# Inverse transforms along x of three images: one product of folded columns in place of two

## The chip, the cores and the metric

The kernel runs on one core of a Trainium2 chip. Its time is the device time of one execution in microseconds (us). The median of three runs of the kernel before is 10099.33 us (10097.6 to 10100.59). All arrays are 32-bit floats.

A core has five engines with instruction queues of their own: TensorE (PE) multiplies matrices, with its weight loads shown apart (PEld); VectorE (DVE), ScalarE (ACT) and GpSimd (POOL) work element by element; SyncE (SP) issues nearly all transfers between the chip's main memory and the core's on-chip memory. Products land in a separate accumulator memory of eight banks, called PSUM.

## The reference

Four images x of 128 channels and 128 x 128 pixels go through two layers. The first is a selective state-space layer over windows of 8 x 8 pixels. The second is a Fourier layer; only that one is touched:

```python
z = layer norm of x over the channels
Xf = jnp.fft.rfft2(z, axes=(-2, -1))                      # 128 x 65 frequencies
Uf = Xf[:, :, None, :, :] * jnp.conj(Phi)[None, None]     # 16 complex masks Phi_l
U = jnp.fft.irfft2(Uf, s=(gx, gy), axes=(-2, -1))
S = jnp.einsum('bdlxy,lhd->bhxy', U, Theta)
H = gelu(W1 S + b1)
out = W2 H + b2
return x + out
```

The kernel mixes channels before it transforms back: for each frequency it forms the sum over l of conj(Phi_l) times Theta_l Xf, and applies the inverse transform to that sum, one image of 128 channels at a time.

## The kernel before, in words

**Stages.** One core does everything in sequence: the state-space layer (0 to 7120 us, `mamba_layer`), the forward transforms (`spectra`, to 7420), the mixing with Theta and Phi (`mix`, to 9294), and then, image by image, the inverse transforms and the MLP (`images_and_mlp`, to the end). The order of instructions on each engine is that in which the program writes them; inside these stages there is no planner. SP too works strictly in order: a transfer whose source isn't ready, or whose buffer isn't free, holds up every transfer written after it.

**Mixing.** A row is one y frequency y of the 65 (KY). For each of 16 masks k, `products` multiplies the row's spectrum `xk` (columns of x frequencies as weights) by Theta_k (line 621), so that the results have the x frequency on the 128 partitions and image by channel along the free axis. Real and imaginary parts are then scaled by Phi, one number per partition, and added to `acc` (line 649 on DVE, lines 636 and 638 on ACT and POOL for the masks of `APART`). `COLS` says which x frequency each partition holds: frequencies 0 to 31, then the mirror images of 0 to 31 (128 minus the frequency, and 64 in place of the mirror image of 0), then 32 to 63, then their mirror images. So partition 32 + i holds the mirror image of partition i, and 96 + i that of 64 + i. `finish` stores each row to main memory in `sf` (line 659), 8 transfers a row: four images by two halves of the channels.

**Images and MLP.** For one image, `load_spectrum` brings the mixed spectrum back (x frequency on partitions; y frequency, real or imaginary part, channel along the free axis). `reorder` copies 16 channels at a time into `so`, laid out as minus imaginary, real, imaginary (lines 710 to 712). `along_x` transforms along x: for each channel two products are added in PSUM, one with the cosines `ix[:, :W]` (line 721) and one with the sines `ix[:, W:]` (line 722). The weights are the channel's spectrum (128 x 128) and the results have 128 y numbers (65 real and 63 imaginary parts) on partitions and the pixel x along the free axis. Four channels share a PSUM bank; ACT and DVE take turns copying banks into `px` (line 724). When all 128 channels are through, the image goes on in 32 steps of four pixels x. Each step k has `along_y` (line 735, product with `idft_y`, copied by DVE, line 736), `hidden` (line 743, W1, and line 744, gelu on ACT) and `project` (line 752, W2, and line 753, where DVE adds the bias and the layer's input). The steps are staggered: step k writes `along_y` of k + 1, `hidden` of k and `project` of k - 1. Every second step loads eight rows of the layer's input `mx` (line 730), and every second `project` stores eight rows of the result (line 755). The spectrum of the next image is loaded in two halves, one in the middle of `along_x`, one in step 0 of the MLP.

Of the kernel before, what the change touches and what calls it, by code (L numbers as in the profile page):

```python
# [13 lines left out]
F32 = mybir.dt.float32  # L14
# [20 lines left out]

COLS = np.arange(W // 2).reshape(2, 1, W // 4)
COLS = np.concatenate((COLS, np.where(COLS > 0, W - COLS, W // 2)), 1).reshape(W)


def mamba_layer(tc, d, x, x1, zb, deltas, dus, results):  # L40
# [549 lines left out]
        tc.nc.sync.dma_start(t[:, :, :, q], xf[y // YG][y % YG, :, :, q])  # L590


def mix(tc, theta, phi, xf, firsts, sf, first):

# [8 lines left out]
    with ExitStack() as ctx:  # L603
        ctx.enter_context(tc.manual_schedule())
        sb = ctx.enter_context(tc.tile_pool(name="m_sb", bufs=3, reuse_waits="tile"))
        ps = ctx.enter_context(tc.tile_pool(name="m_ps", bufs=4, space=PSUM, reuse_waits="tile"))
        nc.vector.tensor_scalar(phi[2], phi[1], -1.0, None, ALU.mult)
        rows = {y: SimpleNamespace(xk=t) for y, t in enumerate(firsts)}

# [53 lines left out]
        load(2)  # L663
        for y in range(KY):
# [8 lines left out]
        finish(KY - 1)  # L673


def load_spectrum(tc, sf, b, q, groups, t):
    for g in groups:
        tc.nc.sync.dma_start(t[:, SG[g] : SG[g + 1]], sf[b][g][:, q])


def images_and_mlp(tc, c, sp, spec, sf, x1, out):

    nc = tc.nc
    B = len(sf)
    CG, CB = HB // W, 16
    HP = P // 2
    n = WS * W  # L690
    with ExitStack() as ctx:
        ctx.enter_context(tc.manual_schedule())
        sb = ctx.enter_context(tc.tile_pool(name="i_sb", bufs=2, reuse_waits="tile"))
        ps = ctx.enter_context(tc.tile_pool(name="i_ps", bufs=2, space=PSUM, reuse_waits="tile"))
        ix, iy = c["idft_x"], c["idft_y"]
        ordered, px, rows = {}, {}, {}

        def load(b, q):
            if b < B:
                spec[b, q] = sp.tile([P, KY, 2, HP], F32, tag="s", name="s", bufs=2)  # L700
                load_spectrum(tc, sf, b, q, range(len(SG) - 1), spec[b, q])

        def reorder(b, i):

            if i == P:
                b, i = b + 1, 0
            if b < B:
                s = spec[b, i // HP][:, :, :, i % HP : i % HP + CB]
                t = ordered[b, i] = sb.tile([P, CB, 3 * KY - 2], F32, tag="so", name="so")
                nc.scalar.activation(t[:, :, :KY].rearrange("p c y -> p y c"), s[:, :, 1], AF.Copy, scale=-1.0)  # L710
                nc.vector.tensor_copy(t[:, :, KY : 2 * KY].rearrange("p c y -> p y c"), s[:, :, 0])
                nc.vector.tensor_copy(t[:, :, 2 * KY :].rearrange("p c y -> p y c"), s[:, : KY - 2, 1])

        def along_x(b, i):
            if i % CB == 0:
                reorder(b, i + CB)
                along_x.s = ordered.pop((b, i))
            p1 = ps.tile([P, CG, W], F32, tag="p1", name="p_ix")
            for k in range(CG):
                s = along_x.s[:, i % CB + k]  # L720
                nc.tensor.matmul(p1[:, k], s[:, KY:], ix[:, :W], start=True, stop=False)
                nc.tensor.matmul(p1[:, k], s[:, :P], ix[:, W:], start=False, stop=True)
            to = px[b][:, :, i : i + CG].rearrange("p x c -> p c x")
            (nc.scalar.copy if i % (2 * CG) else nc.vector.tensor_copy)(to, p1)

        def along_y(b, k):
            if k % 2 == 0:
                o = rows[b, k // 2] = SimpleNamespace(at=slice(k * CG, (k + 2) * CG))
                o.x = sb.tile([P, n], F32, tag="mx", name="mx")
                nc.sync.dma_start(o.x, x1[b][:, o.at].rearrange("c x y -> c (x y)"))  # L730
                o.u = sb.tile([P, 2, HB], F32, tag="mu", name="mu")
                o.o = sb.tile([P, n], F32, tag="mo", name="mo")
            p2 = ps.tile([P, CG, W], F32, tag="p2", name="p_iy")
            for q in range(CG):
                nc.tensor.matmul(p2[:, q], px[b][:, k * CG + q], iy, start=True, stop=True)
            nc.vector.tensor_copy(rows[b, k // 2].u[:, k % 2], p2.rearrange("p x y -> p (x y)"))

        def hidden(b, k):
            o = rows[b, k // 2]
            o.g = sb.tile([P, 2, HB], F32, tag="g", name="g")  # L740
            for m in range(2):
                ph = ps.tile([P, HB], F32, tag="ph", name="p_h")
                nc.tensor.matmul(ph, c["W1"][:, m * P : (m + 1) * P], o.u[:, k % 2], start=True, stop=True)  # L743
                nc.scalar.activation(o.g[:, m], ph, AF.Gelu, bias=c["b1"][:, m : m + 1])
            return o.g

        def project(b, k, g):
            o = rows[b, k // 2]
            hs = slice(k % 2 * HB, (k % 2 + 1) * HB)
            po = ps.tile([P, HB], F32, tag="po", name="p_o")  # L750
            for m in range(2):
                nc.tensor.matmul(po, c["W2"][:, m], g[:, m], start=(m == 0), stop=(m == 1))
            nc.vector.scalar_tensor_tensor(o.o[:, hs], po, c["b2"], o.x[:, hs], ALU.add, ALU.add)
            if k % 2:
                nc.sync.dma_start(out[b][:, o.at].rearrange("c x y -> c (x y)"), o.o)

        reorder(0, 0)
        for b in range(B):
            px[b] = sb.tile([P, W, P], F32, tag="px", name="px", bufs=1)
            for i in range(0, P, CG):  # L760
                along_x(b, i)

                if i == HP + CB:
                    load(b + 1, 0)
            along_y(b, 0)
            before = None
            for k in range(W // CG):
                if k + 1 < W // CG:
                    along_y(b, k + 1)
                g = hidden(b, k)  # L770
                if before:
                    project(b, *before)
                before = k, g
                if k == 0:
                    load(b + 1, 1)
            project(b, *before)


# [1 line left out]
def conv_kernel(ctx: ExitStack, tc: tile.TileContext, d, out):  # L780
# [3 lines left out]
    def images(name):  # L784
# [4 lines left out]
    sf = [  # L789
        [tc.dram_tile([W, 2, j - i, 2, P // 2], F32, name=f"sf_{b}_{i}") for i, j in zip(SG[:-1], SG[1:])]  # L790
        for b in range(B)
    ]
# [5 lines left out]
    with ExitStack() as stages:  # L798
        with tc.tile_pool(name="results", bufs=1, side="right") as results:
# [10 lines left out]
            def constants():  # L810
# [5 lines left out]
                m.firsts = [  # L816
                    small([B, 4 * (W // 2)], f"xk{y}").rearrange("p b (r q x) -> p b r q x", r=2, q=2) for y in range(2)
                ]

            def first_rows():  # L820
                for y, t in enumerate(m.firsts):
# [1 line left out]

            spectra(tc, d, zb, xf, zp, stores, constants, first_rows)

        sp = ctx.enter_context(tc.tile_pool(name="sp", bufs=1, side="right", reuse_waits="tile"))
        c = {}
        for k in "idft_x idft_y W1 b1 W2 b2".split():
            c[k] = sp.tile(list(d[k].shape), F32, tag=k, name=f"c_{k}")
            nc.sync.dma_start(c[k], d[k])  # L830
        spec = {(0, q): sp.tile([P, KY, 2, P // 2], F32, tag="s", name="s", bufs=2) for q in range(2)}

        def first_image(g):
            for q in range(2):
                load_spectrum(tc, sf, 0, q, [g], spec[0, q])

        mix(tc, m.theta, m.phi, xf, m.firsts, sf, first_image)
    images_and_mlp(tc, c, sp, spec, sf, x1, out)


def dft():
# [2 lines left out]
    h = w[:, :KY]  # L844

    s = w[:KY] * np.where(np.arange(KY) % (W // 2) == 0, 1, 2)[:, None] / W**2
    parts = {
        "dft_x": (h.real, -h.imag[:, 1:-1]),
        "dft_y": (h.imag, h.real, -h.imag),
        "idft_x": (w.real[COLS], w.imag[COLS]),  # L850
    }
    d = {k: np.concatenate(v, 1).astype(np.float32) for k, v in parts.items()}
    rows = np.r_[1 : KY - 1, 0, KY - 1]
# [15 lines left out]
def layout(i):  # L869
# [17 lines left out]
    d["Phi_r"], d["Phi_i"] = (i[f"L1_conv_Phi_f_{k}"].transpose(1, 0, 2)[COLS] for k in ("real", "imag"))  # L887
# [21 lines left out]
```

## Time and profile before

| | |
|---|---|
| median of three runs | 10099.33 us |
| the profiled execution | 10102.73 us |
| its span, first to last instruction | 10100.2 us |
| state-space layer | 0 to 7120 us |
| forward transforms | 7120 to 7420 us |
| mixing | 7420 to 9294 us |
| images and MLP | 9304 to 10100 us |
| PE busy in the whole span | 9084.8 us (90%) |
| DVE, ACT, POOL | 88%, 64%, 82% |

The profile is of one execution. A group row gives the line, the engine and the operation; what it writes and reads; shapes; how often; then busy time, the mean duration of one, and the engine's idle time just before them with what ended that. Matrix products follow each other so closely that their durations overlap; what one costs is the step from one to the next. A product of 32-bit numbers shows as two records. A stretch row gives busy time and number of instructions of PE, PEld, DVE, ACT and POOL in a window, the clock that PE was granted (1.00 is full), the mean busy share of the 16 DMA engines, and the rate of transfer in GB/s. DMA rows give the size of one transfer and the median time from its issue to its landing.

### The profile page before, as it was taken

Reading aid. Unit: us, or ns where it says so; the run is one execution under the profiler, and the core shown is the slowest. Engines: PE = TensorE matmul, PEld = TensorE weight load, DVE = VectorE, ACT = ScalarE, POOL = GpSimd, SP = SyncE. Lnnn points to the kernel's source line nnn. Section 1 sums busy time; section 2 is a strip of 40 time slices with the busy share of each in tenths; the row PEclk is TensorE's granted clock in tenths of the full one; section 3 lists DMA queues with packets and bytes.
Section 4 is the critical chain, followed back from the end, with each engine's and each line's share of the span. In section 5 each row is a group of like instructions: output and inputs, shape, how many; then the busy total and the mean of one; then the engine's idle time right before and its main releaser. Section 6 shows DMA issues by size and latency. Waiting matters only on the chain.

```text
span 10100.2 us, 142674 instructions
## 1 busy us (share of the span) xinstructions
PE 9084.8 (90%) x47892; PEld 4884.4 (48%) x47892; DVE 8843.0 (88%) x7100; ACT 6493.7 (64%) x12443; POOL 8238.1 (82%) x4259
## 2 busy tenths in 40 slices
PE   7888888888888888888888888888899999999999
PEld 3333333333333333333332333332799999999666
DVE  6999999999999999999999999999579999998333
ACT  5776777777777777777767777776545555554433
POOL 6898899999999989988998999999369999996000
PEclk8899999999999999999999999998899999999999
DMA  5777677777767777777776777777741111111332
GB/s 176 215 227 219 211 229 217 219 219 223 223 214 227 218 215 223 220 220 215 227 221 212 229 219 218 218 221 223 212 116 39 47 37 45 39 47 54 131 128 92
DMA packets 1173229, 1793.97 MB, mean 178 GB/s; under 512 B 369664, under 2 KB 437520, under 8 KB 1169296
## 3 DMA queue, kind: packets, MB, share of 16 engines
q1 hardware_dynamic: 1171920, 1784.71, 58.5%
q8 instruction: 380, 6.23, 0.3%
q14 instruction: 353, 2.89, 0.1%
q10 hardware_dynamic: 576, 0.14, 0.0%
HBM read 1481.41 MB, written 303.04 MB: 177 GB/s over the span
## 4 chain that ended last, share of the span: by engine, by line
PE 65%; ACT 15%; DVE 9%; DMA 6%; issue 3%; SPq 1%; POOL 1%; DVEq 0%; ACTq 0%; POOLq 0%
PE p_v L621 18%; PE p_conv L220 6%; PE p_du L400 6%; DVE hs L434 6%; DMA dr<-delta 5%; PE p_dt L245 5%; PE p_bc L235 5%; PE p_y L452 5%; DVE p_du L432 3%; ACT dA L415 3%; PE p_out L292 2%; PE ln_cen L169 2%; ACT cs L176 2%; ACT p_du L415 2%; PE p_h L743 2%
## 5 line engine op out<-in xcount | busy, mean ns | idle before, releaser
L442 POOL TENSOR_TENSOR hs<-hs,bc 128x1024 f32<-128x1024 f32 x2048 | 4811.0, 2377 | 398.0 <-DVE hs L434 347.3
L434 DVE TENSOR_TENSOR_SCAN hs<-dA,p_du 128x1024 f32<-128x1024 f32 x1600 | 3659.2, 2287 | 211.5 <-ACT dA L415 8.9
L432 DVE TENSOR_TENSOR p_du<-p_du,bc 128x1024 f32<-128x1024 f32 x1600 | 1936.3, 1210 | 194.2 <-PE p_du L400 189.5
L415 ACT ACTIVATE dA<-dr,A 128x504 f32<-128x504 f32 x3200 | 2071.7, 704 | 35.2 <-DVE hs L434 24.1
L621 PE MATMUL p_v<-theta,xk 128*128 128x128 f32 x16640 | 1864.0, 275 | 16.3 <-DMA xk<-xf 11.8
L621 PEld LDWEIGHTS p_v<-theta,xk 128*128 128x128 f32 x16640 | 1861.1, 192 | 19.2 <-issue 11.9
L649 DVE SCALAR_TENSOR_TENSOR acc<-p_v,phi,acc 128x512 f32<-128x512 f32 x2622 | 1768.0, 744 | 104.4 <-PE p_v L621 80.0
L638 POOL TENSOR_TENSOR acc<-acc,part 128x512 f32<-128x512 f32 x1408 | 1741.4, 1282 | 117.2 <-ACT part L636 110.5
L400 PE MATMUL p_du<-du,c_rsel 32*128 32x512 f32 x6400 | 1362.0, 677 | 372.1 <-DVE hs L434 371.9
L452 PE MATMUL p_y<-hs,c_ssel 128*32 128x512 f32 x8192 | 1224.6, 633 | 137.8 <-DVE yz L281 83.4
L636 ACT ACTIVATE part<-p_v,phi 128x512 f32<-128x512 f32 x1408 | 891.3, 686 | 578.7 <-PE p_v L621 572.5
L434 DVE TENSOR_TENSOR_SCAN hs<-p_du,ur 128x1024 f32<-128x1024 f32 x448 | 1019.0, 2275 | 79.1 <-ACT p_du L415 58.3
L380 POOL TENSOR_TENSOR ur<-ur,bc 128x1024 f32<-128x1024 f32 x448 | 1064.7, 2377 | 10.5 <-DMA ur<-du 10.5
L220 PE MATMUL p_conv<-tn,W_conv 128*128 128x512 f32 x2016 | 991.9, 616 | 0.0
L400 PEld LDWEIGHTS p_du<-du,c_rsel 32*128 32x128 f32 x6400 | 370.3, 192 | 1083.3 <-issue 782.6
L245 PE MATMUL p_dt<-xc,W_dt 128*128 128x512 f32 x1008 | 609.7, 735 | 40.6 <-ACT dl L256 39.2
L415 ACT ACTIVATE p_du<-dr,A 128x504 f32<-128x504 f32 x896 | 613.9, 685 | 29.1
L452 PEld LDWEIGHTS p_y<-hs,c_ssel 128*32 128x32 f32 x8192 | 184.1, 111 | 890.6 <-issue 565.9
L225 ACT ACTIVATE xc<-p_conv,b_conv 128x512 f32<-128x512 f32 x252 | 173.5, 688 | 625.8 <-PE p_conv L220 625.8
L220 PEld LDWEIGHTS p_conv<-tn,W_conv 128*128 128x128 f32 x2016 | 341.6, 189 | 446.3 <-issue 244.3
L263 POOL TENSOR_TENSOR dl<-dl,ab 128x1024 f32<-128x1024 f32 x128 | 302.8, 2365 | 299.1 <-ACT ab L260 299.1
L235 PE MATMUL p_bc<-xc,c_W_bc 128*128 128x512 f32 x1008 | 493.3, 612 | 36.0 <-ACT dl L256 36.0
(133 smaller groups left out, 9683.8 us busy)
## 6 DMA issues: line engine op xcount, KB each, us to landing
dr<-delta SPq DMA_DIRECT2D x4096, 256.0 KB, 5.2
ur<-du SPq DMA_DIRECT2D x896, 256.0 KB, 6.4
delta<-dl SPq DMA_DIRECT2D x128, 512.0 KB, 2.9
du<-du SPq DMA_DIRECT2D x128, 512.0 KB, 5.4
xf<-x SPq DMA_DIRECT2D x40, 832.0 KB, 8.8
xk<-xf SPq DMA_DIRECT2D x130, 256.0 KB, 3.7
sf<-acc SPq DMA_DIRECT2D x520, 64.0 KB, 1.7
xt<-in_x_dram SPq DMA_DIRECT2D x64, 512.0 KB, 7.4
```

What stands on the lines that cost most here:

```text
L220: nc.tensor.matmul(windows(o.pc), W_conv[:, ch, k], moved, start=(k == 0), stop=(k == K - 1))
L245: nc.tensor.matmul(o.pd, W_dt[:, k, ch * P : (ch + 1) * P], half(o.xc[:, k], h), start=(k == 0), stop=(k == 1))
L380: nc.gpsimd.tensor_tensor(fetched[s], fetched[s], both(o.bc[0], h), ALU.mult)
L400: nc.tensor.matmul(u.bank[:, j % 2], c["rsel"][p, u.i], half(u.o.du[p, u.ch], u.h), start=True, stop=True)
L415: nc.scalar.activation(u.dA[:, q, :, 1:], u.delta[:, q].rearrange("p (w t) -> p w t", t=L)[:, :, 1:], AF.Exp, scale=A[:, g : g + 1],)
L432: nc.vector.tensor_tensor(u.bu, u.bu, both(u.o.bc[0], u.h), ALU.mult)
L434: nc.vector.tensor_tensor_scan(u.hs.rearrange("p q t -> p (q t)"), u.dA.rearrange("p q w t -> p (q w t)"), u.bu.rearrange("p q t -> p (q t)"),
L442: nc.gpsimd.tensor_tensor(u.hs, u.hs, both(u.o.bc[1], u.h), ALU.mult)
L452: nc.tensor.matmul(o.py[h, ch][32 * j : 32 * j + 32], c["ssel"][:, u.i], units[s + j // 2].hs[:, j % 2], start=(u.i == 0), stop=False, ski ...
L621: nc.tensor.matmul(t[:, b], o.xk[:, b, r], theta[:, k], start=True, stop=True)
L638: nc.gpsimd.tensor_tensor(into, into, part, ALU.add)
L649: nc.vector.scalar_tensor_tensor(into, v, factor, into, ALU.mult, ALU.add)
```

## The change

A real image has a spectrum whose parts at a frequency and at its mirror image enter the same cosine and sine. For the images after the first, the two products along x are replaced by one. Its weights, `folded`, are sums of two terms: the real part of a column and the imaginary part of its mirror image, and so on, with signs. The matrix `ix[:, :W]` then holds cosines on the partitions of frequencies up to 64 and sines on those of the mirror images.

- *Phi.* On the mirrored partitions Phi_r and Phi_i change places, and a new input `sign` (+1 or -1 per partition) multiplies `phi[0]` at the start of `mix`, so that those partitions hold the spectrum times i, up to sign.
- *Stores.* The first image's two stores a row are unchanged. Those of images 1 to 3 go to new tensors `sf_b`, each [128, 4, 2, 65, 32]: quarter of the channels, real or imaginary, y frequency, 32 channels. There are still 8 transfers a row.
- *Loads.* In steps 0, 3, ..., 21 of an image's MLP, `load` brings one piece (a quarter q of the next image's channels, part r) as one transfer of 128 partitions into `s`, and part 1 - r of the same quarter, with mirrored partitions exchanged, into `mirrors[r]` as four transfers of 31, 31, 32 and 32 partitions. Partitions 0 and 32 have no partner and stay zero. Each partition's row is 65 x 32 numbers, 8,320 bytes, in one piece.
- *Folds.* Three steps later `fold` adds or subtracts the two on GpSimd and writes the result, with y frequency along the innermost axis, into `folded`, 128 channels by 128. The two parts of a quarter make 65 and 63 columns.
- *Images 1 to 3* have no `reorder`. The first image still has its two products and its reorders.
- *Memory.* `along_x` uses all eight PSUM banks in turn, the MLP writes its result into the tile that holds its input (three buffers, `mo` is gone), and pools are closed and opened after the first image's transforms. The constants of the last stage get a pool of their own; their six loads then stand on SP ahead of the stores of the first image's forward spectrum instead of behind those of the last.

```diff
+MIRROR = COLS > W // 2
+HQ = 32
...
+        nc.vector.tensor_scalar(phi[0], phi[0], sign, None, ALU.mult)
         nc.vector.tensor_scalar(phi[2], phi[1], -1.0, None, ALU.mult)
...
-                for b in range(B):
-                    for q in range(2):
-                        hs = slice(q * (P // 2), (q + 1) * (P // 2))
-                        nc.sync.dma_start(sf[b][g][:, q, at - SG[g]], o.acc[:, b, :, hs])
-                    if b == 0 and y in [k if k < KY else KY - 1 for k in SG[1:]]:
-                        first(g)
+                for q in range(2):
+                    hs = slice(q * (P // 2), (q + 1) * (P // 2))
+                    nc.sync.dma_start(sf[0][g][:, q, at - SG[g]], o.acc[:, 0, :, hs])
+                if y in [k if k < KY else KY - 1 for k in SG[1:]]:
+                    first(g)
+                for b in range(1, B):
+                    for r in range(2):
+                        nc.sync.dma_start(sf[b][:, :, r, at], o.acc[:, b, r].rearrange("p (q h) -> p q h", h=HQ))
...
+        def load(b, i):
+            if b < B and i < 2 * (P // HQ):
+                q, r = divmod(i, 2)
+                s[i] = late.tile([P, KY, HQ], F32, tag="s", name="s")
+                nc.sync.dma_start(s[i], sf[b][:, q, r])
+
+                for to, of in ((0, 32), (32, 0), (64, 96), (96, 64)):
+                    at = int(to < 64)
+                    nc.sync.dma_start(mirrors[r][to + at : to + 32], sf[b][of + at : of + 32, q, 1 - r])
+
+        def fold(b, i):
+            if b < B and 0 <= i < 2 * (P // HQ):
+                q, r = divmod(i, 2)
+                k = KY - 2 * r
+                to = folded[:, q * HQ : (q + 1) * HQ, r * KY : r * KY + k].rearrange("p c y -> p y c")
+                nc.gpsimd.tensor_tensor(to, s.pop(i)[:, :k], mirrors[r][:, :k], ALU.add if r else ALU.subtract)
+
         def along_x(b, i):
-            if i % CB == 0:
-                reorder(b, i + CB)
-                along_x.s = ordered.pop((b, i))
-            p1 = ps.tile([P, CG, W], F32, tag="p1", name="p_ix")
+            if b == 0 and i % CB == 0:
+                reorder(i + CB)
+                along_x.s = ordered.pop(i)
+
+            bank = ("p1", "p2", "ph", "po")[i // CG % 4]
+            p1 = ps.tile([P, HB], F32, tag=bank, name="p_ix").rearrange("p (c x) -> p c x", x=W)
             for k in range(CG):
-                s = along_x.s[:, i % CB + k]
-                nc.tensor.matmul(p1[:, k], s[:, KY:], ix[:, :W], start=True, stop=False)
-                nc.tensor.matmul(p1[:, k], s[:, :P], ix[:, W:], start=False, stop=True)
+                if b:
+                    nc.tensor.matmul(p1[:, k], folded[:, i + k], ix[:, :W], start=True, stop=True)
+                else:
+                    t = along_x.s[:, i % CB + k]
+                    nc.tensor.matmul(p1[:, k], t[:, KY:], ix[:, :W], start=True, stop=False)
+                    nc.tensor.matmul(p1[:, k], t[:, :P], ix[:, W:], start=False, stop=True)
...
-                o.x = sb.tile([P, n], F32, tag="mx", name="mx")
+                o.x = sb.tile([P, n], F32, tag="mx", name="mx", bufs=3)
...
-            nc.vector.scalar_tensor_tensor(o.o[:, hs], po, c["b2"], o.x[:, hs], ALU.add, ALU.add)
+            nc.vector.scalar_tensor_tensor(o.x[:, hs], po, c["b2"], o.x[:, hs], ALU.add, ALU.add)
...
+            if b == 0:
+                early.close()
+                done()
+                late = ctx.enter_context(tc.tile_pool(name="i_late", bufs=2, reuse_waits="tile"))
+                folded = late.tile([P, P, P], F32, tag="folded", name="folded", bufs=1)
+                for r in range(2):
+                    mirrors.append(late.tile([P, KY, HQ], F32, tag=f"sm{r}", name="sm", bufs=1))
+                    nc.gpsimd.memset(mirrors[r], 0.0)
             along_y(b, 0)
             before = None
             for k in range(W // CG):
+                if k % 3 == 0:
+                    fold(b + 1, k // 3 - 1)
+                    load(b + 1, k // 3)
...
-        "idft_x": (w.real[COLS], w.imag[COLS]),
+        "idft_x": (np.where(m, -w.imag[COLS], w.real[COLS]), np.where(m, w.real[COLS], w.imag[COLS])),
...
+    m = MIRROR[:, None, None]
+    d["Phi_r"], d["Phi_i"] = np.where(m, j, r), np.where(m, r, j)
+    d["sign"] = np.where(MIRROR, -1, 1).astype(np.float32)[:, None]
```

More of the change, by code (lines that the diff above doesn't have):

```diff
@@ L590, in load_row, with mix @@
         tc.nc.sync.dma_start(t[:, :, :, q], xf[y // YG][y % YG, :, :, q])
-def mix(tc, theta, phi, xf, firsts, sf, first):
+def mix(tc, theta, phi, sign, xf, firsts, sf, first):
     nc = tc.nc
@@ L673, in mix, with images_and_mlp @@
         finish(KY - 1)
[L676 to L681, printed above, removed]
+def images_and_mlp(tc, c, spec, done, sf, x1, out):
     nc = tc.nc
@@ L694, in images_and_mlp, with reorder @@
         ps = ctx.enter_context(tc.tile_pool(name="i_ps", bufs=2, space=PSUM, reuse_waits="tile"))
+        early = ExitStack()
+        so = early.enter_context(tc.tile_pool(name="i_so", bufs=2, reuse_waits="tile"))
         ix, iy = c["idft_x"], c["idft_y"]
[L696 to L709, printed above, removed]
+        ordered, px, rows, s, mirrors = {}, {}, {}, {}, []
+        def reorder(i):
+            if i < P:
+                s = spec[i // HP][:, :, :, i % HP : i % HP + CB]
+                t = ordered[i] = so.tile([P, CB, 3 * KY - 2], F32, tag="so", name="so")
                 nc.scalar.activation(t[:, :, :KY].rearrange("p c y -> p y c"), s[:, :, 1], AF.Copy, scale=-1.0)
@@ L728, in along_y @@
                 o = rows[b, k // 2] = SimpleNamespace(at=slice(k * CG, (k + 2) * CG))
-                o.x = sb.tile([P, n], F32, tag="mx", name="mx")
+                o.x = sb.tile([P, n], F32, tag="mx", name="mx", bufs=3)
                 nc.sync.dma_start(o.x, x1[b][:, o.at].rearrange("c x y -> c (x y)"))
                 o.u = sb.tile([P, 2, HB], F32, tag="mu", name="mu")
-                o.o = sb.tile([P, n], F32, tag="mo", name="mo")
-            p2 = ps.tile([P, CG, W], F32, tag="p2", name="p_iy")
+            p2 = ps.tile([P, HB], F32, tag="p2", name="p_iy").rearrange("p (x y) -> p x y", y=W)
             for q in range(CG):
@@ L752, in project @@
                 nc.tensor.matmul(po, c["W2"][:, m], g[:, m], start=(m == 0), stop=(m == 1))
-            nc.vector.scalar_tensor_tensor(o.o[:, hs], po, c["b2"], o.x[:, hs], ALU.add, ALU.add)
+            nc.vector.scalar_tensor_tensor(o.x[:, hs], po, c["b2"], o.x[:, hs], ALU.add, ALU.add)
             if k % 2:
-                nc.sync.dma_start(out[b][:, o.at].rearrange("c x y -> c (x y)"), o.o)
-        reorder(0, 0)
+                nc.sync.dma_start(out[b][:, o.at].rearrange("c x y -> c (x y)"), o.x)
+        reorder(0)
         for b in range(B):
@@ L761, in images_and_mlp @@
                 along_x(b, i)
-                if i == HP + CB:
-                    load(b + 1, 0)
+            if b == 0:
[6 more added lines that the diff above has]
+                    nc.gpsimd.memset(mirrors[r], 0.0)
             along_y(b, 0)
@@ L773, in images_and_mlp @@
                 before = k, g
-                if k == 0:
-                    load(b + 1, 1)
             project(b, *before)
@@ L788, in conv_kernel @@
     xf = [tc.dram_tile([min(YG, KY - y), P, B, 2, 2, W // 2], F32, name=f"xf_{y}") for y in range(0, KY, YG)]
[L789 to L792, printed above, removed]
+    sf = [[tc.dram_tile([W, 2, j - i, 2, P // 2], F32, name=f"sf_{i}") for i, j in zip(SG[:-1], SG[1:])]]
+    sf += [tc.dram_tile([W, P // HQ, 2, KY, HQ], F32, name=f"sf_b{b}") for b in range(1, B)]
     deltas, dus = (
@@ L815, in constants @@
                 nc.sync.dma_start(m.phi[1], d["Phi_i"])
-                m.firsts = [
-                    small([B, 4 * (W // 2)], f"xk{y}").rearrange("p b (r q x) -> p b r q x", r=2, q=2) for y in range(2)
-                ]
+                m.sign = small([1, 1], "sign")[:, 0]
+                nc.sync.dma_start(m.sign, d["sign"])
+                firsts = small([2, B * 4 * (W // 2)], "xk01")
+                m.firsts = [firsts[:, y].rearrange("p (b r q x) -> p b r q x", b=B, r=2, q=2) for y in range(2)]
             def first_rows():
@@ L824, in conv_kernel @@
             spectra(tc, d, zb, xf, zp, stores, constants, first_rows)
-        sp = ctx.enter_context(tc.tile_pool(name="sp", bufs=1, side="right", reuse_waits="tile"))
+        cp = ctx.enter_context(tc.tile_pool(name="i_const", bufs=1, side="right", reuse_waits="tile"))
+        sp = ExitStack()
+        pool = sp.enter_context(tc.tile_pool(name="sp", bufs=2, side="right", reuse_waits="tile"))
         c = {}
         for k in "idft_x idft_y W1 b1 W2 b2".split():
-            c[k] = sp.tile(list(d[k].shape), F32, tag=k, name=f"c_{k}")
+            c[k] = cp.tile(list(d[k].shape), F32, tag=k, name=f"c_{k}")
             nc.sync.dma_start(c[k], d[k])
-        spec = {(0, q): sp.tile([P, KY, 2, P // 2], F32, tag="s", name="s", bufs=2) for q in range(2)}
+        spec = [pool.tile([P, KY, 2, P // 2], F32, tag="s", name="s") for q in range(2)]
         def first_image(g):
             for q in range(2):
-                load_spectrum(tc, sf, 0, q, [g], spec[0, q])
-        mix(tc, m.theta, m.phi, xf, m.firsts, sf, first_image)
-    images_and_mlp(tc, c, sp, spec, sf, x1, out)
+                nc.sync.dma_start(spec[q][:, SG[g] : SG[g + 1]], sf[0][g][:, q])
+        mix(tc, m.theta, m.phi, m.sign, xf, m.firsts, sf, first_image)
+    images_and_mlp(tc, c, spec, sp.close, sf, x1, out)
 def dft():
@@ L846, in dft @@
     s = w[:KY] * np.where(np.arange(KY) % (W // 2) == 0, 1, 2)[:, None] / W**2
+    m = MIRROR[:, None]
     parts = {
@@ L886, in layout @@
     d["Theta"] = i["L1_conv_Theta"].transpose(2, 0, 1)
-    d["Phi_r"], d["Phi_i"] = (i[f"L1_conv_Phi_f_{k}"].transpose(1, 0, 2)[COLS] for k in ("real", "imag"))
+    r, j = (i[f"L1_conv_Phi_f_{k}"].transpose(1, 0, 2)[COLS] for k in ("real", "imag"))
+    m = MIRROR[:, None, None]
+    d["Phi_r"], d["Phi_i"] = np.where(m, j, r), np.where(m, r, j)
+    d["sign"] = np.where(MIRROR, -1, 1).astype(np.float32)[:, None]
     d["W1"], d["W2"] = i["L1_conv_W1"].T, col(i["L1_conv_W2"].T)
```

## The prediction

> **What bounds the kernel now.** I read the busy shares first, then the stages by windows, then the chain of waits of the last 800 us, the groups of instructions and the DMA rows. All times are of the profiled execution: 10102.73 us with a span of 10100.2; the median of the runs is 10099.33, so a difference in the span carries over to the median as it is.
>
> The change acts on the last stage, images and MLP, 9304 to 10100 us. The windows give it image by image (columns: window; length; busy time of PE, PEld, DVE, ACT, POOL with instruction counts; PEclk; DMA share; GB/s):
>
> ```profile
> 9503.00:9562.00 59.00, 57.78 (x513) 57.29 (x511) 33.30 (x33) 30.89 (x23) 0.00 (x0) 1.00 0.42 165
> 9562.00:9700.00 138.00, 137.98 (x511) 77.16 (x512) 45.41 (x63) 45.81 (x65) 0.00 (x0) 1.00 0.34 114
> ```
>
> An image is 59 us of transforms along x and 138.5 us of transforms along y with the MLP. PE is busy throughout at full clock, DVE and ACT about half or a third, GpSimd (POOL) never. The chain agrees; only PE lines have weight in it:
>
> ```profile
> by line: PE p_h L743 27.2%; PE p_o L752 27.1%; PE p_iy L735 14.2%; PE p_ix L721 13.7%; PE p_ix L722 13.6%; issue 0.7%; DVE acc L649 0.7%; ACT px L724 0.5%; DVE px L724 0.4%; DVE so L711 0.4%; DVE mo L753 0.4%; DMA s<-sf 0.4%; DMA sf<-acc 0.
> ```
>
> ```profile
> L721 PE MATMUL p_ix<-c_idft_x,so 128*128 128x128 f32 x1024 | 199.7, 277 | 15.6 <-DVE so L712 15.2
> L722 PE MATMUL p_ix<-c_idft_x,so 128*128 128x128 f32 x1024 | 199.1, 276 | 0.0
> L724 DVE COPY px<-p_ix 128x512 f32<-128x512 f32 x64 | 68.2, 1065 | 77.3 <-PE p_ix L722 75.3 <-issue 2.0
> L724 ACT COPY px<-p_ix 128x512 f32<-128x512 f32 x64 | 67.7, 1057 | 115.3 <-PE p_ix L722 115.3
> ```
>
> The means of 277 ns overlap one another, so busy time divided by count is no price. The price is the step: 512 records fill about 57.5 us, 0.112 us each, two records to a matmul, 0.224 us a matmul.
>
> **What is removed.** Images 1 to 3 lose the second product, L722: 128 matmuls an image. 128 x 0.224 = 28.6 us an image, 3 x 28.6 = 86 us, on the path. The copies out of PSUM keep up: two engines take 1.06 us each for every second group, and a group of four matmuls then takes 0.9 us. Their drain at the end of the stage (PE waits 1.1 us an image for ACT px) stays. The reorders of images 1 to 3 (L710 to L712, 2.19 us on ACT and 1.16 + 1.15 on DVE per 16 columns) lay under PE: 0.
>
> **What is added and costs nothing, with its cover.**
> - 24 folds on GpSimd. The row of 1024 elements takes 2377 ns (L442), that of 512 takes 1282 (L638), so 2080 elements come to about 4.6 us; by the strided row (L552, 390 elements, 1028 ns) 5.5. I take 5. A fold falls due every third step of 4.33 us, every 13 us, on an idle engine. DVE does not suffer beside a busy GpSimd: the L649 operation takes 744 ns while GpSimd is 93% busy (1741 of the mixing stage's 1874 us), its like in the MLP (L753) 751 with GpSimd idle.
> - Two memsets before the first mirror load: no row for them; between 0 and 5 us each by the fold, and SP, which holds image 0's next loads, waits behind them. The MLP's own loads queued behind them are wanted two to three steps later (9 to 13 us): 0, at most 10.
> - One scaling of phi[0] on DVE (1.19 us as phi[2]), before a first product that DVE waits 11.45 us for: 0. Constants loaded earlier, in SP's idle time: 0.
> - The mixing stage keeps 8 stores a row of frequencies, six of them in pieces of 128 bytes instead of 256. DMA share there is 0.19, PE waited for xk only once, and rows are loaded three ahead. Even doubled it stays hidden: 0, at most 2 us.
> - In-place MLP output with three buffers: a load waits for a store three rows (26 us) older, and stores land in 2.9 us: 0 as long as the queue isn't late.
>
> **What is added and is not free: the loads.** Per image 8 pieces, each of one 128-row transfer and four mirror transfers, of 31, 31, 32 and 32 rows, every row 8,320 bytes, during MLP steps 0, 3, ... 21. By volume they fit: 2.1 MB per 13 us is 164 GB/s beside the 114 of the MLP, and this trace reaches 358:
>
> ```profile
> 9550.00:9560.00 10.00, 10.00 (x92) 10.00 (x92) 4.98 (x5) 5.19 (x4) 0.00 (x0) 1.00 0.93 358
> ```
>
> By these rows alone the loads are hidden and the sum is -86 us. A rule of the Trainium skill speaks against it: "DMA: Bandwidth & Descriptors", section "Why a DMA increments its semaphore by 16 and not by 1". A transfer is dealt to k of the 16 engines, k being the largest number up to 16 that divides the slowest dimension of both sides, and a hardware queue takes the lowest-numbered k. 128 and 32 rows give 16. 31 is prime: one engine, the same for both transfers of each piece and for every later one. Before has no odd count, but two small loads have 8 rows, in the first 40 us:
>
> ```profile
> q1 hardware_dynamic: 2192, 1.61, 14.9%
> ```
>
> Fifteen 128-row loads and two of 8 rows make 1936 data packets; with one completion packet per engine used, 15 x 16 + 2 x 8 = 256 more give exactly 2192, while 16 engines for the small ones would give 2208. So the number of engines follows the rows; that 31 means one, no run here shows. I take the rule.
>
> **What that engine then has to carry.** The trace's packet records have a median of 309 ns for 8,192 bytes (mean 343, first packets being slow) and 159 ns for 4,096. So an 8,320-byte row takes 0.314 to 0.348 us, and the 62 rows of the two odd transfers 19.5 to 21.6 us; I take 20. The engine's part of the other three transfers is 8 + 2 + 2 rows, 3.8 us: 23.8 us a piece, against 13 us between pieces. The MLP's own loads and stores (8 rows of 4,096 bytes each) add 1.27 us apiece.
>
> Who waits: SP issues in order, and each engine serves in order. The load of mx issued behind a piece lands only when this engine is through with the piece; L753's successor on DVE waits for mx, the next mu copy stands behind it on DVE, and so does PE's next hidden product. The out store waits for DVE, and SP holds the next piece behind it.
>
> ```profile
> mx<-x SPq DMA_DIRECT2D x64, 512.0 KB, 4.4
> L753 DVE SCALAR_TENSOR_TENSOR mo<-p_o,c_b,mx 128x512 f32<-128x512 f32 x128 | 96.1, 751 | 344.0 <-PE p_o L752 344.0
> ```
>
> Today mx lands in 4.4 us and DVE waits for PE alone; the slack is about 3 steps, 12 us, which 23.8 us of backlog exceeds. Then the engine sets the pace:
> - image 0: 8 x 23.8 = 190; 22 loads and stores up to step 21, 28 us; the mx behind the last piece is wanted in step 23, after it 9 steps, 39 us. Total 257 instead of 138.5: +119.
> - images 1 and 2: piece 0 already runs under the transform along x, -23.8: 234, +95 each.
> - image 3 loads nothing: 0.
>
> +309 - 86 = +223. PE then idles over 10 us at a time and restarts slowly: after the 15 us gap at 9288 the granted clock is 0.60 over 9300 to 9310. Some 2 us an image of that lie on the path, 7 us. +230 us: 10099 + 230 = **10330 us**.
>
> **The rivals.**
> 1. *The odd transfers are spread after all* (two rows to an engine). Then a piece costs an engine under 5 us, the loads hide, and -86 remains: 10014 us. For it: the volume row above. Against it: the rule. With x us for the two odd transfers on the busiest engine, the three MLPs grow by 3 x (8(x + 3.8) + 67 - 138.5) - 2(x + 3.8) = 22x - 131; this equals 86 at x = 9.9. Below that the change is faster.
> 2. *Two engines share them*, x near 10: the gain is just given back, about 10100, 10060 to 10140.
> 3. *GpSimd is the bound.* A fold would have to take over 13 us, 2.4 times the dearest row; at 20 us each, +7 us a fold and 24 folds, less 86: 10180. Only a stride penalty unlike L552's would do it.
> 4. *The change doesn't remove the product*: not possible here, the second matmul is absent for images 1 to 3.
>
> **How the numbers follow.** The single engine 0.84; spread 0.11; two engines 0.04; GpSimd 0.01. Within the likeliest the row price moves x from 19.5 to 21.6: 22 x -0.5 = -11 to 22 x 1.6 = +35 us; what SP's order leaves of slack, and slow restarts, I can only bound by half a piece an image, 3 x 12 = 36 us either way. Its own range is 10280 to 10400. Widened to 10210 to 10450 it holds all but a few per cent of the likeliest case, some 0.81 in all; the spread case is left out below. About 0.2% (20 us) is what a measurement of this kernel tells from no change. Faster: 0.11 + 0.015; same: 0.01; the rest slower.
>
> **What would show it.** Right: landing of the 31-row mirror loads (and mx) in tens of microseconds; DVE's add of x1 waiting for DMA mx, PE idle in the MLP windows of images 0 to 2 and none in image 3; MLP windows near 257, 234, 234 and 138 us; DMA share in them low, near 0.35, though DMA is the limit; transforms along x at 30 us from image 1 on; folds near 5 us. Wrong: 31-row loads landing within 5 us or PE solid there (rival 1), GpSimd solid (rival 3), or a mixing stage longer than 1874 us, which I put at nothing.

## The result, and the profile after

| | median of the runs, us | range, us | against before |
|---|---|---|---|
| before | 10099.74 | 10097.60 to 10100.59 | 1 |
| after | 10365.19 | 10355.12 to 10370.85 | 1.0262 (95% interval 1.0244 to 1.0280) |

The changed kernel is 2.6% slower; 10330 was predicted, with a range of 10210 to 10450. The profiled execution of after has a span of 10363.2 us, 263 more than before. All of it arises in the last stage: the matmuls of the mixing stage (L626, L621 before) took 1864.2 us against 1864.0, and the first product along x starts at 9301.3 us against 9303.8. In the experiments below, each ratio is against runs of before that were made beside that experiment (medians of 10101.73 and 10100.29 us).

These are the windows of after over that stage:

```profile
9362.00:9619.00 257.00, 157.42 (x511) 84.21 (x512) 43.43 (x63) 45.14 (x65) 36.39 (x8) 0.79 0.36 119
9619.50:9649.50 30.00, 29.03 (x258) 28.60 (x256) 17.45 (x17) 16.57 (x16) 0.00 (x0) 1.00 0.40 122
9650.00:9904.00 254.00, 155.17 (x512) 83.52 (x511) 43.46 (x63) 43.97 (x64) 36.38 (x8) 0.80 0.36 119
9934.00:10190.00 256.00, 156.38 (x513) 84.16 (x514) 43.45 (x63) 43.97 (x64) 36.39 (x8) 0.79 0.36 118
10220.00:10363.00 143.00, 138.67 (x512) 77.03 (x511) 46.16 (x64) 43.97 (x64) 0.00 (x0) 1.00 0.34 111
```

Row 2 is a transform along x with one product: 30 us where before took 59. Rows 1, 3 and 4 are the transforms along y with the MLP of images 0 to 2, which load the mirrors of the next image. They take 257, 254 and 256 us where before took 138, and PE is idle for 100 us of each. In the last image, which loads nothing, PE is solid again (row 5 runs on to the end of the span, 4 us past PE's last product). The DMA share of the slow windows is 0.36, so an average over the 16 engines shows nothing near a limit.

The chain that ended last, by line, over the same stage:

```profile
by line: DMA sm<-sf_b 47.4%; PE p_h L763 10.2%; PE p_o L772 9.8%; PE p_ix L739 7.7%; DMA mx<-x 7.2%; PE p_iy L755 4.8%; PE p_ix L742 2.7%; PE p_ix L743 2.7%; SPq L721 1.3%; ACT px L745 0.4%; issue 0.4%; DVE mx L773 0.3%; DVE mu L756 0.2%; A
```

Before, only PE lines had weight here. Now almost half of the stage is the landing of mirror loads. The groups of instructions name the receivers of that wait (busy time and mean in ns, then idle time before them and what ended it):

```profile
L739 PE MATMUL p_ix<-c_idft_x,folded 128*128 128x128 f32 x768 | 86.2, 275 | 0.0
L763 PE MATMUL p_h<-mu,c_W 128*128 128x512 f32 x512 | 279.5, 674 | 298.0 <-DVE mu L756 297.7 <-ACT g L764 0.4
L773 DVE SCALAR_TENSOR_TENSOR mx<-p_o,c_b,mx 128x512 f32<-128x512 f32 x128 | 96.0, 750 | 707.9 <-DMA mx<-x 451.7 <-PE p_o L772 256.2
L728 POOL TENSOR_TENSOR folded<-s,sm 128x2080 f32<-128x2080 f32 (+1 forms) x24 | 109.2, 4548 | 697.9 <-DMA sm<-sf_b 636.4 <-PE p_iy L755 61.5
```

Before, the line of L763 was L743, and it never waited:

```profile
L743 PE MATMUL p_h<-mu,c_W 128*128 128x512 f32 x512 | 241.3, 594 | 0.0
```

Read the four lines of after from the bottom: GpSimd waits 636 us for mirrors but works only 4.55 us a fold, so it is not the bound. DVE waits 452 us for `mx`, which before it never did (344 us, all for PE). PE waits 298 us for the `mu` copy that stands behind that add on DVE. The image's own rows are late because they are queued behind the mirrors. The DMA rows of the stage:

```profile
q1 hardware_dynamic: 25584, 117.32, 34.9%
...
mx<-x SPq DMA_DIRECT2D x63, 512.0 KB, 27.3
...
sm<-sf_b SPq DMA_DIRECT2D x48, 260.0 KB, 27.5
sm<-sf_b SPq DMA_DIRECT2D x48, 251.9 KB
```

`mx` lands 27.3 us after its issue (median), against 4.4 before. The 27.5 us are those of the 32-row mirrors, which are issued behind the 31-row ones; for the 31-row ones (251.9 KB) the profile gives no landing.

**How many engines.** The packets answer it, by the prediction's way of counting. The stage issues 64 stores, 63 loads of `mx` and 24 of `s`, 128 rows each; 48 mirrors of 32 rows; and 48 of 31. That is (64 + 63 + 24) x 128 + 48 x 32 + 48 x 31 = 22352 data packets. The row of 25584 leaves 3232 others, which are the small ones that the page counts under 512 bytes. With one per engine used, the 199 transfers of 128 or 32 rows give 199 x 16 = 3184, and 48 are left: one for each transfer of 31 rows. On 16 engines they would have given 768.

That both run on the same engine, the packet records show. Here is the first piece of the stage, issued at 9349.7 us, when the other engines are through with it:

```profile
9362.00:9372.00 10.00, 9.63 (x45) 6.26 (x46) 3.05 (x5) 3.92 (x5) 0.00 (x0) 1.00 0.07 29
```

A DMA share of 0.07 is about one engine in 16. From 9360 to 9375.5 us the records hold rows of 8,320 bytes strictly one behind the other, 0.314 us each. One small packet stands at 9365.8 and the next 31 rows later, at 9375.5: the ends of the two odd transfers. Then come twice two rows and a small packet, this engine's part of the two 32-row transfers, and only then, up to 9378.0, its eight rows of `mx`, which had been issued at 9352.5. So one engine carries both odd transfers, in the order of issue. That it is the lowest-numbered one, as the prediction took it, no run here shows.

### The profile page after: what moved, and what is told of

The parts are those of the page before. It is cut to its first block, busy times and chain, and to the rows that moved or that the text cites. A ratio compares the mean times of both kernels' runs of the same rounds, so it can differ in the third digit from the quotient of the medians.

```text
span 10363.2 us, 141183 instructions
## 1 busy us (share of the span) xinstructions
PE 9043.2 (87%) x47124; PEld 4814.5 (46%) x47124; DVE 8790.1 (85%) x7053; ACT 6440.1 (62%) x12419; POOL 8345.9 (81%) x4285
## 5 line engine op out<-in xcount | busy, mean ns | idle before, releaser
L626 PE MATMUL p_v<-theta,xk 128*128 128x128 f32 x16640 | 1864.2, 275 | 16.0 <-DMA xk<-xf 11.5
L626 PEld LDWEIGHTS p_v<-theta,xk 128*128 128x128 f32 x16640 | 1861.3, 192 | 18.9 <-issue 11.7
L382 POOL TENSOR_TENSOR ur<-ur,bc 128x1024 f32<-128x1024 f32 x448 | 1060.0, 2366 | 10.4 <-DMA ur<-du 10.4
L773 DVE SCALAR_TENSOR_TENSOR mx<-p_o,c_b,mx 128x512 f32<-128x512 f32 x128 | 96.0, 750 | 707.9 <-DMA mx<-x 451.7
L728 POOL TENSOR_TENSOR folded<-s,sm 128x2080 f32<-128x2080 f32 (+1 forms) x24 | 109.2, 4548 | 697.9 <-DMA sm<-sf_b 636.4
L764 ACT ACTIVATE g<-p_h,c_b 128x512 f32<-128x512 f32 x256 | 175.8, 687 | 716.8 <-PE p_h L763 716.4
```

Source lines behind the costliest of these rows:

```text
L382: nc.gpsimd.tensor_tensor(fetched[s], fetched[s], both(o.bc[0], h), ALU.mult)
L626: nc.tensor.matmul(t[:, b], o.xk[:, b, r], theta[:, k], start=True, stop=True)
```

## The experiments

### The 31 rows cut into 15 and 16

The theory is that one DMA engine carries each 31-row transfer. Its rival is that the transfers are late for another reason: their volume, GpSimd, or SP's order. Only the cut changes here; the bytes stay.

```diff
                 for to, of in ((0, 32), (32, 0), (64, 96), (96, 64)):
-                    at = int(to < 64)
-                    nc.sync.dma_start(mirrors[r][to + at : to + 32], sf[b][of + at : of + 32, q, 1 - r])
+                    for i, j in ((1, 16), (16, 32)) if to < 64 else ((0, 32),):
+                        nc.sync.dma_start(mirrors[r][to + i : to + j], sf[b][of + i : of + j, q, 1 - r])
```

> The two mirror transfers of 31 rows are each cut into 15 and 16 rows; everything else is the changed kernel. Theory (31 rows run on one DMA engine, and that engine sets the pace of the MLP of images 0 to 2): 15 rows take 15 engines, 16 rows 16, a piece costs the busiest engine 8 + 2 + 2 + 4 rows, 16 x 0.314 = 5 us in 13 us, so the loads hide, PE is solid, MLP windows of 138.5 us, and the saved product shows: 10100 - 86 = 10014 us. Rival (the volume of the loads, their number, or the chain load, fold, load over SP and GpSimd sets the pace): seven transfers a piece instead of five, so 10365 us or more.

Measured: 10013.43 us (10010.05 to 10014.78), 0.9912 of before (0.9898 to 0.9927). It beats both kernels. The first MLP in its windows, and its DMA rows of the last stage:

```profile
9362.00:9500.00 138.00, 137.63 (x514) 77.01 (x513) 45.31 (x63) 44.97 (x66) 33.21 (x8) 1.00 0.73 219
```

```profile
q1 hardware_dynamic: 27024, 117.32, 38.0%
...
mx<-x SPq DMA_DIRECT2D x63, 512.0 KB, 5.7
...
sm<-sf_b SPq DMA_DIRECT2D x48, 260.0 KB, 9.5
sm<-sf_b SPq DMA_DIRECT2D x48, 130.0 KB, 8.5
sm<-sf_b SPq DMA_DIRECT2D x48, 121.9 KB, 8.4
```

The same 117.32 MB now pass at 219 GB/s under a solid PE, and the window is the 138 us of before. The packets over the data are 27024 - 22352 = 4672 = 3184 + 48 x 15 + 48 x 16: the transfer of 15 rows used 15 engines. Volume, the folds on GpSimd and the order on SP are as in after, so none of them costs the 350 us by itself; the number of rows in a transfer does. It is not where a transfer starts either: the transfers of 15 rows begin at partitions 1 and 33, as those of 31 did.

### A 32nd row added

> The 31-row transfers get a 32nd row, so that partitions 0 and 32 receive the row of another frequency instead of staying zero: the two frequencies without a partner are mixed with one they have no part in, all else is computed as before. Same number of transfers, 2 of 126 rows more. Theory of the single engine (32 rows take 16 engines): loads hidden, 10014 us. Rival (number, volume or order of transfers): 10365 us, as nothing of these changes.

```diff
-                    at = int(to < 64)
-                    nc.sync.dma_start(mirrors[r][to + at : to + 32], sf[b][of + at : of + 32, q, 1 - r])
+                    nc.sync.dma_start(mirrors[r][to : to + 32], sf[b][of : of + 32, q, 1 - r])
```

Measured: 10011.98 us (10008.08 to 10015.55), 0.9911 of before (0.9897 to 0.9926). One row more to every odd transfer, with as many transfers as in after, takes 353 us off the kernel. Its DMA queue row of the last stage:

```profile
q1 hardware_dynamic: 26352, 117.72, 36.5%
```

There are 48 rows more, so 26352 - 22400 = 3952 = 3184 + 48 x 16: the same 48 transfers now take 16 engines each. So the gain of the first experiment does not come from having more or smaller transfers.

### One of the two odd transfers kept

```diff
-                    at = int(to < 64)
-                    nc.sync.dma_start(mirrors[r][to + at : to + 32], sf[b][of + at : of + 32, q, 1 - r])
+                    for i, j in ((0, 32),) if to >= 64 else ((1, 32),) if to else ((1, 16), (16, 32)):
+                        nc.sync.dma_start(mirrors[r][to + i : to + j], sf[b][of + i : of + j, q, 1 - r])
```

> One of the two 31-row transfers stays (into partitions 33 to 63), the other is cut into 15 and 16 rows. Theory of the single engine: the period of a piece was 29.2 us in the changed kernel, of which the pair took about 20; with one left it is 19.3 us, still over PE's 13. An MLP takes 14 us to piece 1, 7 x 19.3, and 39 behind the last: 188 us, +50 in each of three images, less 86: +64, 10164 us. By the prediction's own formula (22 x - 131 with x = 10) it would be +3, 10103 us; that formula counts piece 0 as covered. Rival (number or volume of transfers): 10365 us.

Measured: 10174.01 us (10171.44 to 10176.03), 1.0072 of before (1.0057 to 1.0087). The two MLPs in its windows and the load of `mx` in its DMA rows:

```profile
9362.00:9554.00 192.00, 147.85 (x506) 80.19 (x506) 43.28 (x63) 45.14 (x65) 36.38 (x8) 0.88 0.50 158
9585.00:9777.00 192.00, 147.59 (x512) 80.68 (x512) 43.41 (x63) 43.97 (x64) 31.76 (x7) 0.90 0.49 157
```

```profile
mx<-x SPq DMA_DIRECT2D x63, 512.0 KB, 18.0
```

Half of the odd rows costs some 160 of the 352 us by which the three MLPs grew in after, and of the landing of `mx` beyond the 5.7 us of the first experiment it leaves 12.3 of 21.6 us. From this kernel to after, the busiest engine's rows in the odd pair go from 33 (31, and 1 + 1 of the cut one) to 62, and the time by 191 us. In both kernels the first piece of an image is through by about the time at which SP issues the second, so seven pieces an image are on the path: 191 / (21 x 29) = 0.31 us a row, the price in the packet records.

The run came out 10 us above what was expected of it, but 71 us above the prediction's formula with x = 10. In image 1 the MLP begins at 9584.7, piece 1 is issued at 9598.6, the `mx` behind the last piece lands at 9744.0, and the MLP ends at 9777.3: 14 us, then 145 us for seven pieces, then 33 us. The formula has no gap, 7 x 13.8 + 28 = 125 us, and 39 us. So what it lacks in this image is the gap of 14 us before piece 1 and 20 us of dearer pieces, less 6 at the end.

The chain of waits in the midst of these 145 us can mislead (start, length, what):

```profile
9625.96 18.50 DMA mx<-x
9644.47 19.99 DMA mx<-x
9664.71 0.54 issue
9665.25 0.69 DVE mu L756
9666.07 3.75 PE p_h L763 x4
9669.82 1.94 PE p_o L772 x4
9671.76 0.89 PE p_iy L755 x8
9672.66 1.72 PE p_h L763 x4
9674.37 1.73 PE p_o L772 x4
9676.13 0.76 DVE mx L773
9676.91 0.34 SPq L775
9677.34 11.84 DMA s<-sf_b
```

A piece is not issued until an out store in front of it on SP has gone out, and that store waits for 12 us of PE and DVE work which follows the landing of `mx`. It looks as if loading and computing took turns. But the chain names what released each step, not what the DMA engines were doing: over 9671 to 9677, within those 12 us, the DMA share is 0.06 at 27 GB/s, one engine passing rows of an odd transfer that was already queued. From 9599 to 9745 the packet records show no gap of even 1 us in which nothing moves. This fits one engine setting the pace here too, from piece 1 on; the records do not name the engines, so it is not shown for the whole stretch.

### Seventeen rows and fourteen

If the number of engines is the largest divisor up to 16, as the prediction took it from the Trainium skill ("DMA: Bandwidth & Descriptors", "Why a DMA increments its semaphore by 16 and not by 1"), then 17 rows go to one engine though 16 are free. By a rule of size (16 engines from 16 rows on), they would be spread.

```diff
-                    at = int(to < 64)
-                    nc.sync.dma_start(mirrors[r][to + at : to + 32], sf[b][of + at : of + 32, q, 1 - r])
+                    for i, j in ((1, 18), (18, 32)) if to < 64 else ((0, 32),):
+                        nc.sync.dma_start(mirrors[r][to + i : to + j], sf[b][of + i : of + j, q, 1 - r])
```

> As the run with 15 and 16 rows, but the 31 rows are cut into 17 and 14: as many transfers, as many bytes, nearly the same sizes. Theory (the largest divisor up to 16 counts): 17 is prime, so both 17-row transfers of a piece run on one engine, and that engine also has a row of each 14: 36 rows of the mirror pair against 33 in the run with one odd transfer (10174 us), 24 x 3 x 0.314 = 22 us more: 10195 us. Rival (smaller transfers are spread, and any cut near the middle does): 10014 us.

Measured: 10210.73 us (10209.84 to 10217.31), 1.0108 of before (1.0092 to 1.0125). Its DMA queue row of the last stage:

```profile
q1 hardware_dynamic: 26256, 117.32, 35.9%
```

26256 - 22352 = 3904 = 3184 + 48 x 1 + 48 x 14. Seventeen rows used one engine, fourteen used fourteen, as the largest divisor has it and a rule of size does not. Cutting 31 at the 17th row instead of the 15th costs 10211 instead of 10013 us.

### The second product put back

The experiment with 15 + 16 rows, and in addition a second product for images 1 to 3, as many matmuls as before had, taken of the folded columns:

```diff
-                    nc.tensor.matmul(p1[:, k], folded[:, i + k], ix[:, :W], start=True, stop=True)
+                    nc.tensor.matmul(p1[:, k], folded[:, i + k], ix[:, :W], start=True, stop=False)
+                    nc.tensor.matmul(p1[:, k], folded[:, i + k], ix[:, W:], start=False, stop=True)
```

> As the run with 15 and 16 rows, but images 1 to 3 get their second product back: the folded column is also multiplied by the second half of the matrix and added, so their output is not the reference's. All else of the change stays: loads, folds, no reorders, eight banks. Theory: a second product costs 28.6 us an image where PE is the bound, so 10013 + 86 = 10099 us. Rival (part of the gain is from the dropped reorders and the wider use of banks): clearly below 10099.

Measured: 10097.80 us (10094.85 to 10101.31), 0.9998 of before (0.9990 to 1.0007). With the cut alone it was 0.9912, so the second product is worth 0.0086 of 10100, or 87 us, and everything else that the change adds or drops (folds, memsets, extra loads and stores, the in-place output, the reorders) comes to nothing beyond the interval, some 10 us, once the rows are cut.

### The next piece issued earlier

In after, SP's timeline at the start of image 1 shows an empty stretch (start, length, instruction):

```profile
9621.63 0.78 SPq L717 DMA_DIRECT2D s<-sf_b  x1
9622.45 2.66 SPq L721 DMA_DIRECT2D sm<-sf_b  x4
9625.15 0.55 SPq L751 DMA_DIRECT2D mx<-x  x1
9663.03 0.36 SPq L775 DMA_DIRECT2D out_dram<-mx  x1
9663.43 0.43 SPq L717 DMA_DIRECT2D s<-sf_b  x1
```

Piece 0 goes out under the transform along x. Piece 1 goes out 42 us later, since it stands behind the out store of step 2. By the window the DMA engines have nothing to do for 13 us before it:

```profile
9650.00:9663.00 13.00, 13.00 (x61) 8.14 (x60) 4.27 (x6) 4.12 (x6) 4.62 (x1) 1.00 0.01 4
```

Here the 31 rows stay, and piece 1 is issued directly behind piece 0:

```diff
-                if k % 3 == 0:
+                if k == 0:
+                    load(b + 1, 0)
+                    load(b + 1, 1)
+                elif k % 3 == 0:
                     fold(b + 1, k // 3 - 1)
-                    load(b + 1, k // 3)
+                    if k > 3:
+                        load(b + 1, k // 3)
```

> The 31-row transfers stay; piece 1 is issued right behind piece 0, in step 0, instead of in step 3. In the changed kernel's trace the piece issued under the transform of images 1 and 2 is through 14 us before SP issues the next, because SP holds it behind the out store of step 2; so nothing was gained from its early start. Theory: the engine then goes on to piece 1 without that gap, the MLP windows of images 1 and 2 (254 and 256 us) shrink by 11 to 14 us each, image 0's hardly: 10365 - 25 = 10340 us. Rival (the period is set by the chain of fold and load and not by the engine): windows unchanged, 10365 us.

Measured: 10342.93 us (10336.06 to 10346.60), 1.0237 of before (1.0220 to 1.0254), 22 us less than after. The MLP of image 1 in its windows:

```profile
9653.00:9896.00 243.00, 153.52 (x512) 83.17 (x513) 43.43 (x63) 43.97 (x64) 36.38 (x8) 0.82 0.37 122
```

243 us against 254, and 246 against 256 in image 2: the empty stretch was on the path. In this run the packet records show no gap of 1 us from 9625 to 9864, so in image 1 SP's order leaves the DMA engines no further idle time before the last load is through. The other 330 us are untouched by it.

## Why the prediction was right, and where it was off

**Right: one engine sets the pace.** The count of packets, the packet records, the landing times of 27 us and the chain show it, and four kernels that change only the cut of the rows or add one move the time between 10012 and 10211 us. The order of waiting (mirrors, then `mx`, then the add, then the `mu` copy, then PE) is the one that the groups of after show.

**Right: the 86 us.** 28.75 us of matmuls stand in each transform along x of images 1 to 3, and 87 us are what a second product brings back.

**Right: what was put at nothing.** Together it came to nothing beyond some 10 us, by the run with the second product put back. Folds at 4.55 us (5 were taken), two memsets of 1.8 us, and the mixing stage at its old length. The stores in 128-byte pieces land in 2.2 us instead of 1.7, hidden as argued. (The volume row of the prediction counts 256 rows a piece; there are 254, so 163 and not 164 GB/s. Nothing hangs on it.)

**Image 0: 257 predicted, 257.5 measured, from terms that are each a little off.** The chain shows its pieces in a row:

```profile
9377.88 28.67 DMA sm<-sf_b
9406.57 28.84 DMA sm<-sf_b
9435.42 30.70 DMA sm<-sf_b
9466.14 29.62 DMA sm<-sf_b
...
9558.40 26.50 DMA mx<-x
```

Piece 0 was issued at 9349.7, 12 us before the MLP begins at 9362. The engine then worked to 9584.9, when the last `mx` landed: 235 us where 8 x 23.8 + 28 = 218 were predicted, some 29 us a piece in place of 27.3. The rest of the MLP took 34.5 us after that, not 39. So 235 - 12 + 34.5 = 257.5: a piece is dearer by 2, and the early start and the short end make up for it. That the two numbers agree so closely is luck.

**Off: "piece 0 already runs under the transform along x, -23.8: 234".** This is the step that failed, in images 1 and 2, and it is where the 35 us lie by which the forecast was low. They took 254.5 and 255.9 us, 42 more than 2 x 234; the 7 us put down for slow restarts come off that. In image 1, from PE's start at 9649.6: 14.3 us until piece 1 is issued, 206 us for seven pieces and what goes between them (predicted 7 x 23.8 + 28 = 195), 34 us to the end (predicted 39). So of the 42 us in two images, some 29 are the wait for piece 1 and 23 the dearer pieces, less 10 at the ends. Piece 0 was hidden as predicted, but its cover did not shorten the rest by all of it, since SP held piece 1 behind the out store of step 2. The prediction had named that hold ("SP holds the next piece behind it") and bounded it by half a piece, but left it out of the sum. The experiment with the earlier issue gives back 22 us of it. Why a piece is dearer was not tested. A candidate is the price of its first packets: the prediction had a mean of 343 ns beside the median of 309 in before, and in the MLP of image 0 of after the 8,320-byte rows have a median of 0.314 us and a mean of 0.40.

**Off: the formula 22x - 131 and its break-even of 9.9 us.** At x = 10 it gives +89, and the kernel with one odd transfer measured +160 (10174 less 10100, and the 86 saved). Its shape is wrong: the credit for piece 0 grows with x, while the wait for piece 1 is 14 us in both kernels. An estimate from the two traces: an MLP is 14 us to piece 1, seven pieces of x + 10.3 us (29.6 measured at 62 rows of 0.314 us, 20.8 at 33), and 34 us to the end. Three of them grow by 3 x (14 + 7(x + 10.3) + 34 - 138.5) = 21x - 55, which gives +354 at x = 19.5 (+352 measured) and +163 at x = 10.4 (+160). It equals the 86 us saved at x = 6.7, some 21 rows: the kernel gives its gain back at fewer rows than the prediction had it, and no run lies there to check it. Seventeen rows (36 on the busiest engine, x = 11.3) should then be at +182 and measured +197; what the other 15 us are stays open.

**The slow restarts of 7 us** cannot be told apart from the waits around them: the windows show PE at a granted clock of 0.79 and 157 us busy for work of 138, but part of that lies in time that PE would have waited anyway.

## What to carry to other kernels

Before a load is cut by the shape of the data, look at its row count: 31 or 17 rows were carried by one DMA engine here, 14 and 15 by as many as they have rows, 16, 32 and 128 by 16. The 31 rows were mended by one more row or by a cut into 15 + 16, and not by one into 17 + 14. A mean DMA share of 0.36 can hide an engine that is full; the packets left over after the data are counted show how many engines a transfer used, and the packet records whether one engine passes its rows alone. And when a queue is served in order, price a late load by what stands behind it, and check when the next transfer can be issued before taking its cover as won. A chain of waits shows what released each step; whether an engine stood still meanwhile has to be looked up.

## What had not been expected

The loss was forecast, and what mends it came out near what each run's text had expected. What stands out is how little decides. One number turned a gain of 0.9% into a loss of 2.6%: leaving out one row of 32 cost 353 us (10365 against 10012), though it moves fewer bytes. And of the two ways to cut 31 rows in about half, 15 + 16 and 17 + 14, the second costs 197 us more. The prediction had not expected that the early start of piece 0 in images 1 and 2 would bring so little: the piece itself is free, but the next one waits 14 us to be issued. Nor did the lone engine slow down: 0.314 us a row of 8,320 bytes when it runs alone, the same as the median of all such rows in the MLP of image 0, so that the loss is one of sharing out and not of slow rows.
